# A sparse graph network on one core: the array of S in four instead of two, panels scattered twice, self-loop sums in PSUM

## The chip, the cores and the metric

The kernel runs on one core of one Trainium2 chip. The metric is the device time of one execution in microseconds. The core has a matrix engine (TensorE, PE in the profile, with its weight loads as PEld), a vector engine (VectorE, DVE), a scalar engine (ScalarE, ACT), a general engine (GpSimd, POOL) and a queue of transfers (SyncE, SP). POOL also issues the indirect transfers, which gather or scatter rows by a list of indices. Each engine works through its own instructions in order and waits at semaphores.

## The reference

Four layers over 32 sequences `x` of 512 nodes and 256 features, with one adjacency matrix `adj` (512 x 512, some 1.5% of it off zero, and the diagonal). Layers 0 and 3 are the costly ones, of this form (weights of their own):

```python
pre_u = einsum('bud,dk->buk', h_t, W1[:d])
pre_v = einsum('bvd,dk->bvk', h_t, W1[d:])
hidden = relu(pre_u[:, :, None, :] + pre_v[:, None, :, :] + b1)
S = sigmoid(einsum('buvk,ko->buvo', hidden, W2)[..., 0] + b2[0])
a_t = einsum('buv,bud->bvd', S * A_a, h_t)
m_t = einsum('uv,bud->bvd', A_m, h_t) * h_t
z_t = beta1*h_t + beta2*(a_t @ Wa + ba) + beta3*(m_t @ Wm + bm)
```

Layer 1 is `z + relu((adj @ z) @ W.T + b)`, layer 2 an attention over all nodes with `adj` added to the logits. `S` is multiplied by `adj`, so it is wanted only where `adj` is not zero.

## The kernel before

The kernel counts the edges of `adj` and takes a sparse path where they are few enough, as here. It works on groups of four sequences (`NB`), eight groups in all, and on the 512 nodes in four chunks of 128 rows (`NC`). For each group and each of the layers 0 and 3:

- `pre` (line 565) computes `pre_u` and `pre_v` with PE for each chunk, adds the bias (line 579, DVE), copies (580, ACT) and stores both to a `table` in DRAM, one row of 1024 numbers (four sequences) for each node and side. It also forms the sum for the node's edge to itself: line 582 adds both sides into the tile `both` in SBUF, line 583 takes relu, weights and sums to `self_s`.
- `edges` (line 616) takes the other edges in 36 items of 128 edges, one edge per partition. For each chunk there are eight items (`OWN`): the k-th edge of each row. Rows with more than eight edges put the rest into panels, two for each half of the rows (`PANELS`): lines of edges of any row in that half. For an item, POOL gathers the other node's rows (`rows`, line 612). The own node's rows (`mine`) come by one plain load for a chunk (line 652, SP) or, for a panel, by another gather (655). DVE adds the two (691), and then either DVE sums with relu and weights in four pieces (707) or DVE does relu and weights in one piece (699) and ACT sums (677). After every four items come exp (ACT, 597), the rest of the sigmoid (DVE, 601 and 602), the product with `adj` (641), and then one put for each item: POOL scatters 128 x 4 numbers to their places in `cells` (606).
- `cells` is the dense `S * adj` in DRAM, zeroed once. The edges stay the same for all groups, so the same places are written again. It is two arrays for each layer, one for each half of the rows (256 x 512 places of four sequences, then spare places for lanes that hold no edge). Consecutive puts into one array are ordered: a put waits until the last put into the same array has landed. `put` (665) picks the next ready item of the other half where there is one. The self loops go to the diagonal by one plain transfer for each half (636).
- `load` (726) reads `cells` back, 1 MB for each chunk, into the tiles `SA`; line 814 copies out one sequence at a time for PE (845) in layer 0, and line 1006 uses it in layer 3.

`middle` (793) is layer 0's end, layers 1 and 2 and the `pre` of layer 3 for the four sequences of a group, `last` (1021) the end of layer 3. The pieces of all these are woven together by times given in units of one `middle` (`weave` and `sparse_path`); while the middle of one group runs, the layer-3 edges of the last group and the layer-0 edges of the next one take turns. An `edges` fetches its first three items ahead (`LEAD`; five in the first and last group), and up to six more pieces (`TAIL`) put what is left at its end. Below that a scheduler fixes the order on each engine.

The order of the items (232 to 240): four of chunk 0, then pairs of chunks 0 and 2, 2 and 1, 1 and 3, and at the end chunk 3 by turns with the four panels. Three tiles hold `mine`. A tile can only be filled again when its last reader is done.

Of the kernel before, what the change touches and what calls it, by code (L numbers as in the profile page):

```python
# [16 lines left out]
P = 128  # L17
# [14 lines left out]
LEAD = 3  # L32
LEAD_AT_ENDS = 5
TAIL = 6
CELLS = HALF * N
ITEMS = NC * OWN + 2 * PANELS
SPARE = NC // 2 * OWN * P + LINES
GROUP = NB * D
HELD = 8

# [179 lines left out]
class Edges:  # L220
# [3 lines left out]
    def __init__(self, m, pool):  # L224
        nc = self.nc = m.nc
        self.m = m
        self.iu = pool.tile([P, 2 * PANELS], I32, name="iu")
        self.iv, self.cell = (pool.tile([P, ITEMS], I32, name=n) for n in ("iv", "cell"))
        self.value = pool.tile([P, ITEMS], F32, name="value")
        self.inode = pool.tile([P, 2 * PANELS], I32, name="inode")  # L230

        order = [item_of(0, j) for j in range(OWN // 2)]
        for lead, other in ((0, 2), (2, 1), (1, 3)):
            for j in range(OWN // 2):
                order += [item_of(lead, OWN // 2 + j), item_of(other, j)]
        tail = [panel_of(h, q) for h in range(2) for q in range(PANELS)]
        for j in range(OWN // 2):
            order.append(item_of(3, OWN // 2 + j))
            order += tail[j : j + 1]
        self.order = order  # L240

    def value_of(self, j):
        k = self.order.index(j)
        return self.value[:, k : k + 1]

    def half_of(self, j):
        return j // OWN // 2 if j < NC * OWN else (j - NC * OWN) // PANELS

    def build(self, counts, adjT, lists, psum, big, tmp):

# [3 lines left out]
        def sheet(n):  # L254
# [23 lines left out]
        nc.gpsimd.iota(row, [[0, 2], [P, 2]], 0, 1, allow_small_or_imprecise_dtypes=True)  # L278
        nc.vector.tensor_scalar(row, row, float(N), None, ALU.mult)
        spare = sheet(NC * OWN)  # L280
        nc.gpsimd.iota(
            spare, [[0, 2], [OWN * P, 2], [P, OWN]], CELLS, 1, allow_small_or_imprecise_dtypes=True
        )
        rows = []
        for _ in range(2):
# [30 lines left out]
        for c in (0, 2, 1, 3):  # L316
            if c == 1:

                pu = psum()[:, 0 : 2 * PANELS]
                ones_bf = bf2[:, 1024:1025]  # L320
                nc.vector.memset(ones_bf, 1.0)
                for k in range(2 * PANELS):
                    h, q = divmod(k, PANELS)
                    mm(nc, pu[:, k : k + 1], [(full[:, h * 2 + c, q * P : (q + 1) * P], ones_bf) for c in range(2)])
                u, node, slot, start, sp, vp, therep, tp = (sheet(2 * PANELS) for _ in range(8))
                nc.vector.tensor_scalar(u, pu, float(HALF - 1), None, ALU.min)
                nc.vector.tensor_copy(node, u)
# [6 lines left out]
                nc.vector.tensor_scalar(sp, slot, float(CELLS + NC // 2 * OWN * P), None, ALU.add)  # L334
# [51 lines left out]
    def slots(self, js, v, there, t, start, spare, off=None):  # L386
# [7 lines left out]
        if off is None:  # L394
            nc.vector.scalar_tensor_tensor(t, v, start, spare, ALU.add, ALU.subtract)
        else:
            nc.vector.tensor_tensor(t, v, start, ALU.add)
            nc.vector.tensor_tensor(t, t, spare, ALU.subtract)
        nc.vector.tensor_tensor(t, t, there, ALU.mult)
        nc.vector.tensor_tensor(self.cell[:, js], t, spare, ALU.add)  # L400

# [17 lines left out]
class Sparse:  # L419
# [3 lines left out]
    def __init__(self, ctx, m, counts, xr, outr, B):  # L423
# [4 lines left out]
        self.dram = pool("dram", 1, space=bass.MemoryType.DRAM)  # L428

        self.cells = {  # L430
            k: [self.dram.tile([CELLS + SPARE, NB], F32, name=f"cells_{k}{q}") for q in range(2)] for k in "03"
        }
        self.lists = self.dram.tile([N, 2 * N], F32, name="lists")
        self.x2s = self.dram.tile([B, P, NC, D], F32, name="x2s")
# [103 lines left out]

    def zeros(self, cells):
        for c in cells:  # L540
            flat = c[0:CELLS, :].rearrange("(q p a) b -> q p (a b)", q=4, p=P)
            for q in range(4):
                self.nc.gpsimd.dma_start(flat[q], self.zero)

    def setup_behind(self):
# [19 lines left out]
    def pre(self, g, b, hT):  # L565
# [3 lines left out]
        for c in range(NC):  # L569
# [8 lines left out]
            puv = self.small.tile([P, 2, D], F32, name="puv", bufs=3)  # L578
            nc.vector.tensor_tensor(puv[:, 0, :], pp[:, 0:D], w["b1bc"], ALU.add)  # L579
            nc.scalar.copy(puv[:, 1, :], pp[:, D:])  # L580
            both = self.small.tile([P, D], F32, name="both", bufs=1)
            nc.vector.tensor_tensor(both, pp[:, D:], puv[:, 0, :], ALU.add)
            nc.vector.scalar_tensor_tensor(
                both, both, 0.0, w["W2bc"], ALU.max, ALU.mult, accum_out=g.self_s[:, c, b : b + 1]
# [19 lines left out]
    def put(self, g, half, at, s):  # L604

        self.nc.gpsimd.indirect_dma_start(  # L606
            out=g.cells[half], out_offset=bass.IndirectOffsetOnAxis(ap=at, axis=0), in_=s, in_offset=None
        )

    def fetch(self, rows, g, at):  # L610
# [5 lines left out]
    def edges(self, g, spare=()):  # L616
# [12 lines left out]
        def own_1():  # L629
            self.sigmoid_of(own)  # L630
            diag = self.counts.diag.unsqueeze(2).to_broadcast([P, NC, NB])
            nc.vector.tensor_tensor(g.self_s, g.self_s, diag, ALU.mult)
            for q in range(2):
                diagonal = g.cells[q][q * HALF : q * HALF + HALF * (N + 1), :]
                diagonal = diagonal.rearrange("(c p a) b -> p c a b", p=P, a=N + 1)[:, :, 0, :]
                nc.sync.dma_start(diagonal, g.self_s[:, 2 * q : 2 * q + 2, :])

        def run_1(ks):
            self.sigmoid_of(g.s[:, ks, :].rearrange(flat))
# [1 line left out]
            nc.vector.tensor_tensor(g.s[:, ks, :], g.s[:, ks, :], value, ALU.mult)  # L641
            for k in range(ks.start, ks.stop):
                j = e.order[k]
                ready.append((e.half_of(j), e.cell[:, j : j + 1], g.s[:, k, :]))

        def fetch(n):
            j = e.order[n]
            c = j // OWN
            if c >= NC or c not in mine:
                t = self.gath.tile([P, GROUP], F32, name="mine", bufs=3)  # L650
                if c < NC:
                    nc.sync.dma_start(t, places[c, 0])
                    mine[c] = t
# [10 lines left out]

        def put():

            at = next((n for n, r in enumerate(ready) if r[0] != self.half), 0)
            if ready:
                r = ready.pop(at)
                self.half = r[0]  # L670
                self.put(g, *r)

        def sums(k, rows):
# [694 lines left out]
```

## Time and profile before

| | |
|---|---|
| timed runs | 3109.6 us median of 3 (3096.97 to 3116.11) |
| profiled execution | 3114.5 us, of which span 3112.8 us |
| PE busy | 2713.5 us (87%), mean granted clock 0.942 |
| DVE, ACT, POOL busy | 2302.9 (74%), 1337.7 (43%), 1531.2 (49%) |
| puts (line 606) | 576, 686.4 us busy, 747.0 us idle before them |
| gathers of rows (line 612) | 552 and 24, 667.6 and 33.2 us busy |
| DRAM traffic | 679 MB, 218 GB/s over the span |

The span runs from the first to the last instruction of the profiled execution; what lies around it is 1.7 us. "Idle before" is time in which the engine had nothing else to do, put down to what ended it. In the timelines of single engines each line has the start, the duration, the engine, the line of the kernel, the operation with its output and input, the number of merged instructions, and in brackets the idle time before it and what ended that.

### The profile page before, as it was taken

What the parts mean: (1) busy time and instruction counts of PE and PEld (TensorE: products, weight loads), DVE (VectorE), ACT (ScalarE), POOL (GpSimd) and SP (SyncE); (2) the same over time, 40 slices, a digit from 0 to 9 for tenths busy, and PEclk for the clock granted to TensorE, in tenths of its full rate; (3) what the DMA queues carried; (4) which work ended last, traced back from release to release, by engine and by line L of the source; (5) the groups of instructions that cost most, each with busy time, mean ns of one, the idle gap of its engine ahead of it and who ended that gap; (6) DMA issues with size and microseconds to landing.
All of it is one profiled execution on the core that took longest, in us unless ns stands there. A gap on an engine that the chain in (4) does not pass through costs nothing. (4 is left out here: it accounts for less than half of the span.)

```text
span 3112.8 us, 32475 instructions
## 1 busy us (share of the span) xinstructions
PE 2713.5 (87%) x8645; PEld 1639.7 (53%) x8646; DVE 2302.9 (74%) x6027; ACT 1337.7 (43%) x4101; POOL 1531.2 (49%) x1328
## 2 busy tenths in 40 slices
PE   6367878889998899989998899989998899879957
PEld 3133444446654566446654565545654466546636
DVE  6964877888689776988489785888679795772761
ACT  3553454444344433444354442544345343443440
POOL 2561553656345552656346562555436563450461
PEclk9688889999999999999999999999999999999979
DMA  8774657776778757776678766787578766551753
GB/s 278 267 238 151 210 164 242 248 261 214 225 214 293 220 189 227 245 263 216 210 212 258 236 196 211 243 266 234 177 225 273 247 220 200 182 183 49 231 196 115
DMA packets 302719, 679.40 MB, mean 218 GB/s; under 512 B 52672, under 2 KB 170944, under 8 KB 294336
## 3 DMA queue, kind: packets, MB, share of 16 engines
q0 software_dynamic: 122688, 414.40, 42.6%
q1 hardware_dynamic: 160880, 225.62, 22.0%
q10 hardware_dynamic: 18960, 37.24, 3.2%
q8 instruction: 70, 1.15, 0.1%
q14 instruction: 121, 0.99, 0.1%
HBM read 531.12 MB, written 146.01 MB: 218 GB/s over the span
## 5 line engine op out<-in xcount | busy, mean ns | idle before, releaser
L606 POOL DMA_INDIRECT cells<-s,cell x576 | 686.4, 1192 | 747.0 <-DMA cells<-s,cell 388.5
L612 POOL DMA_INDIRECT rows<-table,iv x552 | 667.6, 1209 | 619.9 <-DMA table<-puv 150.5
L691 DVE TENSOR_TENSOR rows<-rows,mine 128x1024 f32<-128x1024 f32 x552 | 667.4, 1217 | 191.7 <-DMA rows<-table,iv 173.3
L677 ACT ACTIVATE rows<-rows 128x256 f32<-128x256 f32 x1088 | 439.8, 407 | 506.6 <-DVE rows L699 477.3
L45 PE MATMUL pst<-adj,h 128*128 128x512 f32 x1024 | 452.6, 594 | 0.3 <-PE pst L946 0.3
L707 DVE SCALAR_TENSOR_TENSOR rows<-rows,L_gnn_W2bc 128x256 f32<-128x256 f32 x1120 | 415.0, 417 | 1.8
L45 PE MATMUL pst<-L_gnn_Wa,hT 128*128 128x256 f32 x1024 | 261.3, 406 | 104.8 <-DMA hT<-xT 56.2
L699 DVE SCALAR_TENSOR_TENSOR rows<-rows,L_gnn_W2bc 128x1024 f32<-128x1024 f32 x272 | 329.7, 1214 | 0.3
L45 PEld LDWEIGHTS pst<-adj,h 128*128 128x128 f32 x1024 | 193.4, 191 | 223.3 <-issue 219.4
L45 PEld LDWEIGHTS pst<-L_gnn_Wa,hT 128*128 128x128 f32 x1024 | 204.8, 205 | 151.8 <-issue 85.1
L45 PE MATMUL pst<-eT,feats 128*128 128x512 f32 x512 | 230.9, 604 | 13.0 <-ACT eT L958 13.0
L866 PE MATMUL pst<-WT,hT 128*128 128x256 f32 x512 | 155.1, 470 | 96.0 <-DVE hT L853 96.0
L45 PE MATMUL pst<-adjT,zW 128*128 128x512 f32 x512 | 227.7, 597 | 3.8 <-ACT zW L870 3.8
L1006 PEld LDWEIGHTS pst<-hWa,SA 128*128 128x128 f32 x896 | 213.8, 328 | 7.7 <-issue 4.1
L1006 PE MATMUL pst<-hWa,SA 128*128 128x256 f32 x896 | 216.8, 398 | 0.0
L814 ACT COPY flat<-SA 128x512 f32<-128x512 f32 x128 | 137.7, 1127 | 165.9 <-PE pst L45 83.7
L677 ACT ACTIVATION_READ_ACCUMULATOR rows<-rows 128x1 f32 x1088 | 205.4, 189 | 0.0
L845 PE MATMUL pst<-flat,hWa 128*128 128x512 f32 x448 | 196.8, 592 | 0.0
L866 PEld LDWEIGHTS pst<-WT,hT 128*128 128x128 f32 x512 | 121.4, 242 | 136.6 <-DVE hT L853 107.1
L579 DVE TENSOR_TENSOR puv<-pst,bc_L_gnn_b 128x256 f32<-128x256 f32 x256 | 104.4, 414 | 95.8 <-DMA table<-puv 58.6
L580 ACT COPY puv<-pst 128x256 f32<-128x256 f32 x256 | 93.5, 370 | 180.6 <-DVE puv L579 162.7
L45 PEld LDWEIGHTS pst<-eT,feats 128*128 128x128 f32 x512 | 97.2, 193 | 127.5 <-issue 109.4
(172 smaller groups left out, 3984.4 us busy)
## 6 DMA issues: line engine op xcount, KB each, us to landing
table<-puv SPq DMA_DIRECT2D x256, 256.0 KB, 5.7
SA<-cells POOLq DMA_DIRECT2D x64, 1024.0 KB, 7.2
h<-in_x_dram SPq DMA_DIRECT2D x64, 512.0 KB, 6.5
mine<-table SPq DMA_DIRECT2D x64, 512.0 KB, 5.5
hT<-xT SPq DMA_DIRECT2D x36, 512.0 KB, 5.0
h<-x2s SPq DMA_DIRECT2D x36, 512.0 KB, 4.4
xT<-hT ACTq DMA_DIRECT2D x32, 512.0 KB, 6.1
x2T<-yT SPq DMA_DIRECT2D x32, 512.0 KB, 5.5
```

Of the source, the lines that this page charges most:

```text
L45: nc.tensor.matmul(out, lhsT, rhs, start=(n == 0), stop=(n == len(pairs) - 1))
L579: nc.vector.tensor_tensor(puv[:, 0, :], pp[:, 0:D], w["b1bc"], ALU.add)
L606: self.nc.gpsimd.indirect_dma_start(out=g.cells[half], out_offset=bass.IndirectOffsetOnAxis(ap=at, axis=0), in_=s, in_offset=None)
L612: self.nc.gpsimd.indirect_dma_start(out=rows, out_offset=None, in_=g.table, in_offset=bass.IndirectOffsetOnAxis(ap=at, axis=0))
L677: self.behind(nc.scalar.activation(part, part, AF.Identity, accum_out=g.s[:, k, b : b + 1]))
L691: self.behind(nc.vector.tensor_tensor(rows, rows, other, ALU.add))
L699: nc.vector.scalar_tensor_tensor(by_entry, by_entry, 0.0, w2, ALU.max, ALU.mult)
L707: nc.vector.scalar_tensor_tensor(part, part, 0.0, w["W2bc"], ALU.max, ALU.mult, accum_out=at)
L814: self.nc.scalar.copy(flat[:, r, :], SA[r][:, :, b])
L845: nc.tensor.matmul(pz, hWa[:, r, cs], flat[:, r, :], start=(r == 0), stop=False)
L866: nc.tensor.matmul(pw[:, at], zT[:, d, cs], m.WT_1[:, d, :], start=(d + k == 0), stop=(d * k == 1))
L1006: nc.tensor.matmul(pz[:, k * D : (k + 1) * D], SA[r][:, cs, b], hWa[:, r, :], start=(r + k == 0), stop=False)
```

## The change

- Each layer's `cells` are four arrays, one for each chunk (128 x 512 places, then spare places). A put waits for the last put into the same chunk. `put` picks, among the ready ones, the array that was put to the longest ago.
- A panel's 128 lines can belong to either chunk of its half. It is put twice, once into each array, with a list of places for each (`cell` and `other_cell`); lanes that belong to the other chunk go to spare places. That makes 40 puts for the 36 items.
- The order of the items: four turns of chunk 0, three of chunks 0 and 2, one of 0, 2, 1, four of 2, 1, 3, one of 1, 3, the first panel, two of 1, 3, the last item of chunk 3, the other three panels.
- The diagonal takes four transfers instead of two. The zeros take as many transfers as before, of the same size.
- Four tiles for `mine` instead of three.
- `both` is no tile of its own any more: the self-loop sum is formed in the bank of PSUM that held `pre_u`.

```diff
-CELLS = HALF * N
+ROWS = P * N
+CELLS = ROWS + OWN * P + LINES
 ITEMS = NC * OWN + 2 * PANELS
-SPARE = NC // 2 * OWN * P + LINES
...
+        self.other_cell = pool.tile([P, 2 * PANELS], I32, name="other_cell")
+        self.lower = pool.tile([P, 2 * PANELS], F32, name="lower")
...
-        order = [item_of(0, j) for j in range(OWN // 2)]
-        for lead, other in ((0, 2), (2, 1), (1, 3)):
-            for j in range(OWN // 2):
-                order += [item_of(lead, OWN // 2 + j), item_of(other, j)]
-        tail = [panel_of(h, q) for h in range(2) for q in range(PANELS)]
-        for j in range(OWN // 2):
-            order.append(item_of(3, OWN // 2 + j))
-            order += tail[j : j + 1]
+        left = {c: [item_of(c, j) for j in range(OWN)] for c in range(NC)}
+        panels = [panel_of(h, q) for q in range(PANELS) for h in range(2)]
+        order = []
+        for turns, chunks in ((4, (0,)), (3, (0, 2)), (1, (0, 2, 1)), (4, (2, 1, 3)), (1, (1, 3))):
+            for _ in range(turns):
+                order += [left[c].pop(0) for c in chunks]
+        order.append(panels.pop(0))
+        while left[1]:
+            order += [left[1].pop(0), left[3].pop(0)]
+        order += left[3] + panels
...
+            upper, other = start, self.lower
+            nc.vector.tensor_tensor(other, there, self.lower, ALU.mult)
+            nc.vector.tensor_tensor(there, there, other, ALU.subtract)
+            nc.vector.scalar_tensor_tensor(upper, t, float(-ROWS), there, ALU.add, ALU.mult)
+            nc.vector.tensor_tensor(self.other_cell, upper, spare, ALU.add)
+            there = other
...
         self.cells = {
-            k: [self.dram.tile([CELLS + SPARE, NB], F32, name=f"cells_{k}{q}") for q in range(2)] for k in "03"
+            k: [self.dram.tile([CELLS, NB], F32, name=f"cells_{k}{q}") for q in range(NC)] for k in "03"
         }
...
-            flat = c[0:CELLS, :].rearrange("(q p a) b -> q p (a b)", q=4, p=P)
-            for q in range(4):
+            flat = c[0:ROWS, :].rearrange("(q p a) b -> q p (a b)", q=2, p=P)
+            for q in range(2):
...
-            both = self.small.tile([P, D], F32, name="both", bufs=1)
+            both = pp[:, 0:D]
             nc.vector.tensor_tensor(both, pp[:, D:], puv[:, 0, :], ALU.add)
...
-            for q in range(2):
-                diagonal = g.cells[q][q * HALF : q * HALF + HALF * (N + 1), :]
-                diagonal = diagonal.rearrange("(c p a) b -> p c a b", p=P, a=N + 1)[:, :, 0, :]
-                nc.sync.dma_start(diagonal, g.self_s[:, 2 * q : 2 * q + 2, :])
+            for c in range(NC):
+                diagonal = g.cells[c][c * P : c * P + P * (N + 1), :].rearrange("(p a) b -> p a b", a=N + 1)
+                nc.sync.dma_start(diagonal[:, 0, :], g.self_s[:, c, :])
...
-                ready.append((e.half_of(j), e.cell[:, j : j + 1], g.s[:, k, :]))
+                s, q = g.s[:, k, :], j - NC * OWN
+                if q < 0:
+                    ready.append((j // OWN, e.cell[:, j : j + 1], s))
+                else:
+                    ready.append((q // PANELS * 2, e.cell[:, j : j + 1], s))
+                    ready.append((q // PANELS * 2 + 1, e.other_cell[:, q : q + 1], s))
...
-                t = self.gath.tile([P, GROUP], F32, name="mine", bufs=3)
+                t = self.gath.tile([P, GROUP], F32, name="mine", bufs=4)
...
-            at = next((n for n, r in enumerate(ready) if r[0] != self.half), 0)
             if ready:
-                r = ready.pop(at)
-                self.half = r[0]
+                r = min(ready, key=lambda r: puts.index(r[0]))
+                ready.remove(r)
+                puts.append(puts.pop(puts.index(r[0])))
                 self.put(g, *r)
...
-        self.half = 1
+        puts = list(range(NC))
...
-            cells = g.cells[c // 2][c % 2 * P * N : (c % 2 + 1) * P * N, :]
+            cells = g.cells[c][0:ROWS, :]
```

More of the change, by code (lines that the diff above doesn't have):

```diff
@@ L229, in __init__ @@
         self.value = pool.tile([P, ITEMS], F32, name="value")
+        self.other_cell = pool.tile([P, 2 * PANELS], I32, name="other_cell")
+        self.lower = pool.tile([P, 2 * PANELS], F32, name="lower")
         self.inode = pool.tile([P, 2 * PANELS], I32, name="inode")
-        order = [item_of(0, j) for j in range(OWN // 2)]
-        for lead, other in ((0, 2), (2, 1), (1, 3)):
-            for j in range(OWN // 2):
-                order += [item_of(lead, OWN // 2 + j), item_of(other, j)]
-        tail = [panel_of(h, q) for h in range(2) for q in range(PANELS)]
-        for j in range(OWN // 2):
-            order.append(item_of(3, OWN // 2 + j))
-            order += tail[j : j + 1]
+        left = {c: [item_of(c, j) for j in range(OWN)] for c in range(NC)}
[8 more added lines that the diff above has]
+        order += left[3] + panels
+        assert len(order) == len(set(order)) == ITEMS
         self.order = order
@@ L244, in value_of @@
         return self.value[:, k : k + 1]
-    def half_of(self, j):
-        return j // OWN // 2 if j < NC * OWN else (j - NC * OWN) // PANELS
     def build(self, counts, adjT, lists, psum, big, tmp):
@@ L277, in build @@
         row = sheet(NC)
-        nc.gpsimd.iota(row, [[0, 2], [P, 2]], 0, 1, allow_small_or_imprecise_dtypes=True)
+        nc.gpsimd.iota(row, [[0, NC]], 0, 1, allow_small_or_imprecise_dtypes=True)
         nc.vector.tensor_scalar(row, row, float(N), None, ALU.mult)
@@ L281, in build @@
         nc.gpsimd.iota(
-            spare, [[0, 2], [OWN * P, 2], [P, OWN]], CELLS, 1, allow_small_or_imprecise_dtypes=True
+            spare, [[0, NC], [P, OWN]], ROWS, 1, allow_small_or_imprecise_dtypes=True
         )
@@ L333, in build @@
                 nc.vector.tensor_scalar(start, u, float(N), None, ALU.mult)
-                nc.vector.tensor_scalar(sp, slot, float(CELLS + NC // 2 * OWN * P), None, ALU.add)
+                nc.vector.tensor_scalar(self.lower, u, float(P), None, ALU.is_lt)
+                nc.vector.tensor_scalar(sp, slot, float(ROWS + OWN * P), None, ALU.add)
                 nc.vector.tensor_scalar(tp, slot, 1.0, None, ALU.add)
@@ L602, in sigmoid_of, with put @@
         self.nc.vector.reciprocal(t, t)
-    def put(self, g, half, at, s):
+    def put(self, g, c, at, s):
         self.nc.gpsimd.indirect_dma_start(
-            out=g.cells[half], out_offset=bass.IndirectOffsetOnAxis(ap=at, axis=0), in_=s, in_offset=None
+            out=g.cells[c], out_offset=bass.IndirectOffsetOnAxis(ap=at, axis=0), in_=s, in_offset=None
         )
```

## The prediction

> **What bounds the kernel now.** I read the page's busy row first, then the costliest groups, then busy time by stretches, then the timelines of POOL, DVE and PE where PE stands still.
>
> ```profile
> PE 2713.5 (87%) x8645; PEld 1639.7 (53%) x8646; DVE 2302.9 (74%) x6027; ACT 1337.7 (43%) x4101; POOL 1531.2 (49%) x1328
> L606 POOL DMA_INDIRECT cells<-s,cell x576 | 686.4, 1192 | 747.0 <-DMA cells<-s,cell 388.5
> L691 DVE TENSOR_TENSOR rows<-rows,mine 128x1024 f32<-128x1024 f32 x552 | 667.4, 1217 | 191.7 <-DMA rows<-table,iv 173.3
> ```
>
> PE is busy for 87%, so all that a change of the edge work can win is PE's remaining 400 us. The 576 puts (line 606) cost POOL 1.19 us each, and POOL stood 388.5 us before them because the previous put into the same array had not landed. DVE's add (line 691) waited 173 us for fetched rows. A period (one group) is some 358 us:
>
> ```profile
> 1050.00:1100.00 50.00, 50.00 (x175) 31.71 (x175) 44.58 (x112) 27.00 (x75) 31.16 (x26) 1.00 0.76 232
> 1300.00:1350.00 50.00, 42.56 (x129) 22.70 (x129) 46.28 (x150) 27.11 (x75) 31.07 (x25) 0.97 0.86 277
> 1350.00:1400.00 50.00, 40.77 (x111) 22.11 (x110) 36.94 (x92) 17.49 (x62) 26.57 (x25) 0.90 0.78 269
> ```
>
> (Window, length, then busy us of PE, PEld, DVE, ACT, POOL, granted clock, DMA share, GB/s.) At 1050 PE is full, whatever POOL waits for. It loses 9 us in 1350 to 1400, where a layer-3 group of edges ends and the next layer-0 group begins. There POOL's queue, DVE and PE read:
>
> ```profile
> 1327.88 1.50 POOL L606 DMA_INDIRECT cells<-s,cell  x1 [0.31 <-DVE puv L579]
> ...
> 1336.18 1.19 POOL L606 DMA_INDIRECT cells<-s,cell  x1 [5.42 <-DMA cells<-s,cell]
> ...
> 1343.40 1.09 POOL L606 DMA_INDIRECT cells<-s,cell  x1 [0.31 <-issue]
> ...
> 1351.02 0.97 POOL L606 DMA_INDIRECT cells<-s,cell  x1 [3.71 <-DMA cells<-s,cell]
> ...
> 1364.06 1.79 POOL L606 DMA_INDIRECT cells<-s,cell  x1 [3.88 <-DMA cells<-s,cell]
> ...
> 1369.24 1.19 POOL L606 DMA_INDIRECT cells<-s,cell  x1 [2.81 <-DMA cells<-s,cell]
> 1372.77 0.98 POOL L606 DMA_INDIRECT cells<-s,cell  x1 [2.34 <-DMA cells<-s,cell]
> 1374.05 1.01 POOL L612 DMA_INDIRECT rows<-table,iv  x1 [0.30 <-ACT hWa L745]
> ```
> ```profile
> 1380.31 1.23 DVE L691 TENSOR_TENSOR rows<-rows,mine 128x1024 f32<-128x1024 f32 x1 [8.75 <-DMA rows<-table,iv]
> ```
> ```profile
> 1382.19 6.58 PE L866 MATMUL pst<-WT,hT 128*128 128x256 f32 x16 [9.23 <-DVE hT L853]
> ```
>
> The waits in brackets, 5.42+3.71+3.88+2.81+2.34 = 18.2 us, hold back the new group's seventh fetch (1374.05); DVE stands 8.75 us for its rows, line 853 stands behind that add in DVE's queue, and PE 9.23 us behind line 853. The same stands at 674, 1023, 1740, 2098 and 2459: PE waits 6.8, 9.5, 9.2, 9.0, 5.0, 8.8, together 48.3 us. The start and the end of the kernel end on the same chain: last puts, load of S, matmul.
>
> ```profile
> 255.15 6.06 PE L845 MATMUL pst<-flat,big 128*128 128x512 f32 x10 [12.58 <-ACT flat L814]
> ```
> ```profile
> 3048.91 2.48 DMA cells<-s,cell
> 3052.16 2.10 DMA cells<-s,cell
> 3055.37 8.73 DMA SA<-cells
> 3064.15 7.77 PE pst L1006 x26
> ```
>
> **The change, part by part.** Sums are made against the profiled execution's 3114.5 us (span 3112.8 and 1.7 around it); the median of the three timed runs, 3109.6, is 4.9 lower, and I subtract from it.
>
> *More puts.* Each of 4 panels goes to two arrays: 40 puts a group for 36, 64 more in all, 1.19 and 0.30 of issue each: 6.0 us a group, 95 us of POOL. Where PE is full (1050 to 1150) this is hidden by PE's own work. It is not at the six changes of group, at the start and at the end, where POOL's queue decides.
>
> *Four arrays.* Which wait goes depends on what lies between two puts into one array. Old: from the last fetch of the old group (1324.85) to the seventh of the new (1374.05) are 22 instructions and 18.2 us of waits; (49.2-18.2)/22 = 1.41 us a step. New queue: 25 steps (four more puts, one own-row gather fewer), 35.3 us. Its puts go 0,3,1,3,1, two fetches, 3,1, fetch, 3,1, fetch, 2, fetch, 0,3,2,1, fetch, 3, load, 3, load, seventh fetch: the leftovers are chunks 1 and 3 by turns, so the chain of two arrays stays. I place each put no earlier than the landing of the previous one into its array, with the landings of the rows above in order (1327.88 to 1336.18 is 8.3 us; then 6.8 to 7.6; 5.2 at the end). Waits: 5.5, 1.1, 3.4, 1.1, 0.1, 3.0, sum 14.2. Total 49.5, less 1.0 because two of the steps are loads of 0.9 us: 48.5 against 49.2. With the queue behind it shorter by as much, a gain of 1 us per change, 6 in all. Bounds: all waits gone, the 48.3 us of PE's waits; none gone, three more steps, 6 x 4.2 = 25 us lost.
>
> Within a group three arrays by turns leave two other puts and a fetch between equal ones, over 4 us, so few waits stay. DVE's waits for rows between start and end sum to 144.6 us; 90.5 are eleven of 7 us and more at group boundaries, so some 50 are short ones. I take a third as put waits (17), half of it felt by PE, which waits for DVE in these stretches: -8 (bounds 0 and -25).
>
> *Start.* From the last own-row gather (209.41) old POOL needs 10 puts, 5 fetches, 4 loads and 16.2 us of waits until 249.1. New: 13 puts, 4 fetches, 4 loads, waits by the same placing 11: two steps more (+2.8), 5 less; and each array is loaded by itself, so that one copy of line 814 follows the last landing where two did (254.00 and 256.46): -2.5. Together -5 (bounds: all waits gone -12, no wait gone +6).
>
> *End.* The last three items are panels, so six puts stand at the end instead of a chain of half-1 puts (1.70, 3.69, 2.26 us of waits). After the last gather 17 puts for 12. The last item's data come sooner, since only one gather of own rows is left for the end where two were (DVE stood 8.4 us for one at 3026). Placed as above the last load goes at 3053.9 against 3055.4: -2 (bounds -9 by the waits of this end and its five more puts, +7 by the puts alone).
>
> *Four own-row tiles.* SP's loads and POOL's panel gathers wait less for a tile; POOL's 2.54 us at 919, 1276, 1636, 2356 is not followed by a PE wait: 0. Two more diagonal DMAs a group on SP (0.37 us of issue), queued ahead of table stores and loads; SP's wait for self_s is the same one: 0. The zeros are the same eight 512 KB writes a layer, and the second list of cells is six DVE instructions of 128x4 at some 0.17 us in a part of the setup that is off the chain: 0.
>
> *Self loops in PSUM.* Lines 582 and 583, 256 each, now write PSUM. No DVE row of this trace writes PSUM; rows that read it cost the same (579: 414 ns, 582: 417; 583 in SBUF: 418). I take 0 for the instruction, +2 us for the bank held until 583 (0.67 us longer at the places where PE waited for 582: 6.2 us in 3 times). Upper bound: 583 starts 0.46 us after 582, whose result it reads, the next independent instruction 0.35 us after 583 (1351.37, 1351.83, 1352.18); if a write to PSUM doubled that 0.11 us, 256 x 0.11 = 28 us of DVE, a third of it where PE waits for DVE, +9.
>
> [...]
>
> [...] The rows above land after 3.5 to 8.3 us. [...] I go by the rows.
>
> Sum: -6 -8 -5 -2 +2 = **-19 us**: 3095.5 on the profiled execution, **3090** on the median.
>
> **Rivals.**
> *The chain breaks altogether.* If landings shorten because fewer puts queue behind fetches, the six stalls (48), the short row waits (17), start (-12) and end (-8) go: 85, 3025. For it: 388.5 us of waits are there to be had. Against: chunks 1 and 3 alternate at the end as the halves did.
> *The longer queue decides (slower).* At each change of group POOL does four puts more ahead of the same fetches. If the waits stay as they were, 6.0 us a group come through six times and at both ends: +48, 3158. It decides from the point where the saved waits fall under the 4.2 us of three steps (I have 18.2-14.2 = 4.0 and 1.0 of shorter steps, so near it). For it: POOL's gaps there are bare 0.30 us, a full queue.
> *Nothing reaches PE.* PE is full over half the span; the stall is passed to the next wait for DVE (line 957 waited 41 us for line 918). 3110.
>
> **How the numbers follow.** Forecast 0.42, chain breaks 0.22, longer queue 0.18, nothing 0.18. The forecast alone spans 3065 to 3115. Measurement tells about 1% (31 us) from no change. Faster: the broken chain 0.22 and 0.28 of the forecast, 0.34. Slower: 0.17, nearly all of the longer queue. Same: 0.49. Range 3030 to 3145: it takes half of either rival.
>
> **What would show it.** After: 640 puts; waits of puts for puts down from 388 to 200-280 us; at the group change DVE's wait for rows 6 to 9 us and PE's wait for line 853's counterpart 7 to 9 us, six times; the two self-loop instructions within 10 ns of before; PE's first matmul of flat near 250; last load of S 1 to 3 us earlier against the end of the fetches. Wrong if those PE waits fall under 3 us (broken chain) or pass 13 (longer queue), or if the PSUM rows grow by 60 ns.

## The result, and the profile after

The changed kernel takes 3120.7 us (median of 18 runs, 3114.78 to 3131.11), the kernel before 3100.8 (18 runs, 3091.73 to 3116.11): ratio 1.0062, 95% interval 1.0049 to 1.0076. Run again later (e16), the ratio was 1.0053 (1.0032 to 1.0073). It is slower by some 0.6%, 20 us, where 20 us of gain were forecast. The profiled execution took 3129.4 us (span 3127.7) against 3114.5 (3112.8).

The page after has these lines:

```profile
PE 2725.3 (87%) x8645; PEld 1650.8 (53%) x8646; DVE 2305.5 (74%) x6032; ACT 1341.0 (43%) x4101; POOL 1595.6 (51%) x1392
L618 POOL DMA_INDIRECT cells<-s,cell x576 | 687.6, 1194 | 545.5 <-DVE s L652 193.0
L707 DVE TENSOR_TENSOR rows<-rows,mine 128x1024 f32<-128x1024 f32 x552 | 666.5, 1215 | 166.8 <-DMA rows<-table,iv 162.2
```

(Lines have moved: the put is 618 now, the fetch 624, the add 707, the matmul that stood behind line 853 is 882 behind 869.) POOL has 64 instructions and 64 us more. DVE's wait for rows is 11 us shorter. The waits of POOL (total us, times, longest) show that the four arrays did what they were made for:

```profile
POOL cells L618 <- DMA cells<-s,cell: 198.0, 96, 5.4
POOL rows L624 <- DVE rows L723: 155.6, 41, 27.7
...
POOL cells L618 <- DMA cells<-s,other_cell: 41.8, 12, 5.8
```

240 us of waits of puts for puts, where 388.5 were. PE gained nothing from it: it stood idle for 402.4 us of its span, against 399.3. The change of group that the prediction read at 1324 to 1382 is here, on POOL, DVE and PE:

```profile
1378.05 0.99 POOL L624 DMA_INDIRECT rows<-table,iv  x1 [0.30 <-issue]
1379.35 0.98 POOL L618 DMA_INDIRECT cells<-s,other_cell  x1 [0.30 <-issue]
1380.33 0.59 POOL L748 DMA_DIRECT2D SA<-cells  x1
1385.22 0.99 POOL L618 DMA_INDIRECT cells<-s,other_cell  x1 [4.30 <-DMA cells<-s,other_cell]
1386.21 0.58 POOL L748 DMA_DIRECT2D SA<-cells  x1
1387.10 1.03 POOL L624 DMA_INDIRECT rows<-table,iv  x1 [0.30 <-issue]
```
```profile
1395.94 1.22 DVE L707 TENSOR_TENSOR rows<-rows,mine 128x1024 f32<-128x1024 f32 x1 [6.68 <-DMA rows<-table,iv]
```
```profile
1399.32 2.93 PE L882 MATMUL pst<-WT,hT 128*128 128x256 f32 x6 [5.15 <-DVE hT L869]
```

Two second puts of panels stand between the fetches of 1378.05 and 1387.10, and the later of them waits 4.30 us for the landing of the earlier second put into its own array. Counting DVE's adds back from 1395.94, the one that waits 6.68 us takes the rows of the fetch at 1387.10; PE stands behind it.

The six changes of group together: PE's waits for line 869 are 5.8, 8.3, 5.2, 7.5, 10.2 and 12.7, sum 49.5 us, against 48.3. In the stretch from 58 to 6 us before each of them POOL waited 10.7 us (mean) for landings, against 18.3, and issued 16 puts, against 12: four puts at 1.1 and 0.3 of issue are 5.6 us.

At the start a load of S follows the last put into its array, and the second puts are last:

```profile
242.62 0.97 POOL L618 DMA_INDIRECT cells<-s,other_cell  x1 [0.30 <-issue]
...
249.50 1.00 POOL L618 DMA_INDIRECT cells<-s,other_cell  x1 [5.31 <-DMA cells<-s,other_cell]
...
253.16 0.54 POOL L748 DMA_DIRECT2D SA<-cells  x1 [1.52 <-DMA cells<-s,other_cell]
```

The last load goes at 253.16, against 249.1, and PE's first matmul of line 882 starts at 271.27, against 264.48. But the profile of e16, the same kernel again, has it 10.2 us earlier than this, and earlier than before (first after, then e16):

```profile
271.27 3.62 PE L882 MATMUL pst<-WT,hT 128*128 128x256 f32 x16
```
```profile
261.11 3.62 PE L882 MATMUL pst<-WT,hT 128*128 128x256 f32 x16
```

There too the second puts stand last and are waited for (3.70 and 4.58 us), so these waits are real, but one profile does not tell whether the start as a whole gained or lost. The end is as uncertain: from the first matmul of line 882 for the last sequence to the end of the span are 264.3 us (265.2 in e16), against 272.0, but e2, with the arrays, order and puts of before, has 265.6. Between start and end 15.9 us were lost (12.1 by e16's profile), and only 1.2 of them in the six waits above.

### The profile page after: what moved, and what is told of

It is laid out like the page before. It is cut to its first block, busy times and chain, and to the rows that moved or that the text cites. A ratio compares the mean times of both kernels' runs of the same rounds, so it can differ in the third digit from the quotient of the medians.

```text
span 3127.7 us, 32472 instructions
## 1 busy us (share of the span) xinstructions
PE 2725.3 (87%) x8645; PEld 1650.8 (53%) x8646; DVE 2305.5 (74%) x6032; ACT 1341.0 (43%) x4101; POOL 1595.6 (51%) x1392
## 5 line engine op out<-in xcount | busy, mean ns | idle before, releaser
L882 PE MATMUL pst<-WT,hT 128*128 128x256 f32 x512 | 162.1, 486 | 107.4 <-DVE hT L869 107.4
L47 PE MATMUL pst<-eT,feats 128*128 128x512 f32 x512 | 232.9, 609 | 12.7 <-ACT eT L974 12.0
```

The costliest lines, as they stand in the source:

```text
L47: nc.tensor.matmul(out, lhsT, rhs, start=(n == 0), stop=(n == len(pairs) - 1))
L882: nc.tensor.matmul(pw[:, at], zT[:, d, cs], m.WT_1[:, d, :], start=(d + k == 0), stop=(d * k == 1))
```

## The experiments

The kernel before took 3100 to 3122 us (medians) from one set of runs to another, so each kernel is compared by its ratio to the runs beside it. The columns behind the ratio are read from the profiles: PE's waits in the six changes of group, and POOL's waits for landings in the stretches before them, as above. They come from one profile each and spread: before, e1 and e2, alike in arrays, order and puts, have 48 to 55 us of PE's waits, and stretches that are counted from the start of PE's wait instead of its end give sums of landings up to 21 us different.

| | arrays | order | a panel is put | us | ratio (95%) | PE, six changes | landings |
|---|---|---|---|---|---|---|---|
| before | 2 | old | once | 3100.8 | 1 | 48.3 | 109.8 |
| changed | 4 | new | twice | 3120.7 | 1.0062 (1.0049-1.0076) | 49.5 | 64.0 |
| e1 | 2 | old | once | 3108.7 | 1.0007 (0.9982-1.0031) | 55.4 | 101.4 |
| e2 | 2 | old | once | 3098.9 | 0.9996 (0.9972-1.0019) | 49.0 | 104.8 |
| e3 | 4 | old | twice | 3171.6 | 1.0218 (1.0181-1.0254) | 79.6 | 90.7 |
| e4 | 4 | new | once | 3071.8 | 0.9899 (0.9866-0.9932) | 27.4 | 41.0 |
| e5 | 2 | new | once | 3149.0 | 1.0141 (1.0106-1.0176) | 74.7 | 82.2 |
| e6 | 4 | new | twice, aside | 3108.6 | 0.9999 (0.9978-1.0020) | 40.5 | 32.7 |
| e7 | 4 | new | twice | 3140.2 | 1.0129 (1.0066-1.0192) | 71.3 | 73.1 |
| e8 | 2 | old | once | 3124.0 | 1.0057 (1.0033-1.0081) | 64.7 | 100.1 |
| e9 | 4 | new | 6 puts of 4 | 3118.8 | 1.0012 (0.9979-1.0045) | 49.1 | 71.7 |
| e10 | 4 | new | 6 puts of 4 | 3127.3 | 1.0038 (1.0011-1.0065) | 51.0 | 43.2 |
| e11 | 4 | old | once | 3061.4 | 0.9808 (0.9760-0.9856) | 35.6 | 78.5 |
| e12 | 4 | new | twice | 3121.9 | 1.0017 (0.9993-1.0041) | 37.5 | 74.5 |
| e13 | 4 | old | twice, aside | 3126.2 | 1.0071 (1.0043-1.0098) | 56.0 | 53.2 |
| e14 | 4 | old | 6 puts of 4 | 3164.3 | 1.0192 (1.0130-1.0253) | 76.5 | 99.4 |
| e15 | 4 | old | 6 puts of 4 | 3187.5 | 1.0282 (1.0252-1.0311) | 79.8 | 109.6 |
| e16 | 4 | new | twice | 3118.4 | 1.0053 (1.0032-1.0073) | 47.3 | 64.7 |
| e17 | 4 | old | 5 panels, once | 3165.1 | 1.0145 (1.0120-1.0170) | 60.2 | 84.1 |
| e18 | 4 | old | 5 panels, once | 3161.4 | 1.0128 (1.0104-1.0151) | 64.4 | 61.2 |

**The self loops in PSUM, and the fourth tile (e1, e2).** Two small parts of the change, put into the kernel before.

```diff
-            both = self.small.tile([P, D], F32, name="both", bufs=1)
+            both = pp[:, 0:D]
...  (e2 also)
-                t = self.gath.tile([P, GROUP], F32, name="mine", bufs=3)
+                t = self.gath.tile([P, GROUP], F32, name="mine", bufs=4)
```

> The kernel before with one part alone: the self-loop sum in PSUM (both = pp[:, 0:D]). Theory P (the PSUM part costs what was measured): DVE's rows that write PSUM are longer (in the changed kernel 430 and 426 ns against 417 and 418, the read of the accumulator 139 against 80) and the bank is held longer, so this alone gives +10 to +20 us, ratio 1.003 to 1.006. Theory Q (POOL's longer queue is the cause): within 3 us of before, ratio 0.999 to 1.001. Theory O (the order of the items is the cause): the same, 0.999 to 1.001.

> The kernel before with the self-loop sum in PSUM and four own-row tiles, arrays and order as before. Theory P: +10 to +20 us from the PSUM part, the fourth tile gives 0 to -5. Theory Q and O: within 5 us of before; POOL's waits for a tile (33 us at the panel gathers) go down and PE does not feel it.

Neither makes a difference that these runs can tell. So PSUM does not explain the 0.6%.

**The order, and the second puts (e3, e4).** e3 takes the changed kernel back to the old order of items; e4 leaves the second put of each panel out, and with it those edges.

```diff
-                    ready.append((q // PANELS * 2 + 1, e.other_cell[:, q : q + 1], s))
```

> The changed kernel with the old order of the items (four arrays, panels put twice, four tiles, PSUM kept). Theory O (the new order, with three panels in a row at the end and own rows loaded earlier, is the cause): back to before, ratio 0.998 to 1.002. Theory Q (64 more puts in POOL's queue are the cause): as slow as the changed kernel or slower, 1.005 to 1.010, because the chunk-3 items at the end wait for each other and the extra puts are still there. Theory P: 1.003 to 1.006.

> The changed kernel without the second put of each panel: 36 puts a group instead of 40. It leaves out the edges of the panels that lie in the upper chunk of each half. Theory Q: the 20 us come back and more, 6 us at each of six changes of group and at both ends, ratio 0.985 to 0.998 to before. Theory O: as slow as the changed kernel, 1.004 to 1.008. Theory P: the same, 1.003 to 1.006.

Without the 64 second puts the kernel is 49 us faster than the changed one by the medians, 51 by the ratios (1.0062 to 0.9899), as theory Q said. The order is the same, and PE's waits in the six changes fall from 49.5 us to 27.4. At the start, where the changed kernel's last load of S goes at 253.16 (245.44 in e16), e4's goes here:

```profile
236.07 1.06 POOL L747 DMA_DIRECT2D SA<-cells  x2 [2.41 <-PE pst L47]
```

and at the change of group only the loads of S stand between two fetches, with waits of 2.32 and 0.64 us for landings, and no put:

```profile
1347.72 0.99 POOL L624 DMA_INDIRECT rows<-table,iv  x1 [0.30 <-issue]
1351.03 1.15 POOL L747 DMA_DIRECT2D SA<-cells  x2 [2.32 <-DMA cells<-s,cell]
1352.82 0.54 POOL L747 DMA_DIRECT2D SA<-cells  x1 [0.64 <-DMA cells<-s,cell]
1353.86 1.16 POOL L624 DMA_INDIRECT rows<-table,iv  x1 [0.49 <-issue]
```
```profile
1366.10 1.23 DVE L706 TENSOR_TENSOR rows<-rows,mine 128x1024 f32<-128x1024 f32 x1 [3.33 <-DMA rows<-table,iv]
```

6.1 us from fetch to fetch instead of 9.1, and DVE waits 3.3 us instead of 6.7. Not all of what POOL saves arrives: the fetch of 1353.86, whose rows this add takes, lands only 12.2 us after its issue, the one of 1387.10 in the changed kernel 8.8 us, the one of 1374.05 before 6.2 us. In these stretches the share of the DMA engines is 1.02, 0.95 and 0.64 (414, 309 and 146 GB/s): this fits a fetch that stands behind the loads of S in the transfers, now that POOL issues them closer together. What the transfers alone cost at a change was not tried.

Of the 50.7 us between the two spans 15.3 lie before the first matmul of line 882 (5.2 against e16's profile), 28.0 between that and the last sequence's (22.1 of them in the six changes), 7.4 in the end.

e3 went the other way than the theory that the new order does harm, and past every range: with the old order the changed kernel is 2.2% slower than the kernel before.

**What the order and the arrays are worth, and what a second put is made of (e5 to e8).** e5 is the kernel before with the new order, the fourth tile and PSUM. e6 sends the second puts to arrays of their own:

```diff
-                    ready.append((q // PANELS * 2 + 1, e.other_cell[:, q : q + 1], s))
+                    ready.append((q // PANELS * 2 + 1, e.other_cell[:, q : q + 1], s, True))
...
-            out=g.cells[c], out_offset=bass.IndirectOffsetOnAxis(ap=at, axis=0), in_=s, in_offset=None
+            out=(g.aside if aside else g.cells)[c], out_offset=bass.IndirectOffsetOnAxis(ap=at, axis=0), in_=s, in_offset=None
```

e7 and e8 let POOL put twice an item in every group, in the changed kernel and in the one before:

```diff
-            for _ in range(2 if spare and len(ready) > 2 else 1):
+            for _ in range(2 if len(ready) > 2 else 1):
```

> The kernel before (two arrays by halves, a panel put once) with the new order of items, the self loops' sums in PSUM and four tiles for own rows; only the four arrays and the second puts of the panels are missing. Theory A (the four arrays are worth about 30 us, which the second puts of the panels then eat): this one gets nothing of it, 3095 to 3115, ratio to the kernel before 0.998 to 1.005, and waits of puts for puts near 380 us. Rival B (the gain that e4 showed is the order's, not the arrays'): 3070 to 3085, ratio 0.990 to 0.995.

> The changed kernel, but the second put of each panel goes into an array of its own, one of four that nothing reads (so the edges of these puts are left out of the result). POOL issues the same 640 puts in the same places; only no put and no load of S waits for the 64. Theory T (the time of POOL for 64 puts more, 1.1 us each and 0.3 of issue, ahead of the fetches at a change of group and ahead of the loads of S at both ends): 3112 to 3125, ratio 1.004 to 1.008. Rival W (it is their waits: the second puts go into arrays whose last put has not landed, 116 us of waits before and behind them): near the kernel that puts panels once, 3072 to 3090, ratio 0.990 to 0.997. By the start of the changed kernel, where 4 puts are 5.6 us and the waits for them 6.8 of the 15 us lost, I expect about half way, 3095.

> The changed kernel, with two puts an item where more than two are ready in every group, not only in the first and the last: POOL issues the same 640 puts, earlier, in the middle of a group where PE is full. Theory L (the leftover puts of a group stand ahead of the next group's fetches, and that is where PE loses): the six waits of PE for line 869 fall from 49.5 us to 20 to 35, the time to 3090 to 3105, ratio 0.996 to 1.001; start and end are as before. Rival S (POOL's puts cost wherever they stand, by the waits for their arrays that now come closer together): 3118 to 3135, ratio 1.005 to 1.011, with more than 240 us of waits of puts for puts.

> The kernel before with the same edit alone. Theory L: the six waits of PE for line 853 fall from 48.3 us to 20 to 35, time 3075 to 3090, ratio 0.991 to 0.997. Rival S: with two arrays an earlier put waits for the one before it, POOL's waits grow past 400 us and push the fetches back within the group: 3100 to 3120, ratio 1.000 to 1.006.

e5: the new order in two arrays costs 1.4%, outside either range: the arrays were worth more than theory A gave them (1.0141 to 0.9899, 2.4% or 75 us), and the order by itself is a loss. e6 lies between its two theories: of the second puts' 1.63% some 1.00% (31 us) are POOL's time, 0.63% (20 us) the waits around them. The 31 us hold what the puts aside still wait for one another (19.5 us in the whole profile), and each part is good to about 12 us. e7 and e8 both lose, as rival S said, e7 more than its range. The profiles show why: what stands at the change of group is not a backlog. In the stretches before the six waits e7 still issues 92 puts (95 in the changed kernel), since by the code the last items' puts become ready only there; they wait more for one another (73 us for 64).

**Fewer second puts, and three tiles (e9, e10, e12).** In e9 and e10 the lines of a half's second chunk are laid from the end of the two panels, so that a half's first panel belongs to one chunk and is put once:

```diff
-            pairs = [(before, counts.lines[:, at])]
-            if c % 2:
-                pairs.append((ones[:, 0:P], counts.lines[:, c - 1 : c]))
-            mm(nc, pb[:, at], pairs)
+            mm(nc, pb[:, at], [(later if c % 2 else before, counts.lines[:, at])])
...
+                if q >= 0 and q % PANELS:
                     ready.append((q // PANELS * 2 + 1, e.other_cell[:, q : q + 1], s))
```

(`later` is `before` less one; the second chunk's `base` gets 256 more.) e9 also puts the twice-put panels ahead of the others. e12 is the changed kernel with `bufs=3` for `mine`.

> A version that computes everything: the changed kernel, with the lines of a half's second chunk laid from the end of its two panels, so that a half's first panel holds lines of its first chunk alone and is put once (the sparse path then needs a second chunk with at most 128 lines); 38 puts a group for 40 and 36. The twice-put panels stand between turns of chunks 1 and 3, the once-put ones last. By the 49 us that e4 gave for 64 puts, 32 puts fewer are worth 24 us: theory N (the number counts): 3090 to 3102 with the kernel before at 3104, ratio 0.995 to 0.999. Rival E (the puts that stand last count for more than the others, since every array's last put is what a load of S waits for): 3072 to 3088, ratio 0.990 to 0.995.

> The same, also computing everything, with the panels where the changed kernel has them: one early, three last, so that the last three items give five puts instead of six, and the early one gives one. Theory N: within 6 us of e9, 3090 to 3102, ratio 0.995 to 0.999. Rival E: 10 to 20 us above e9, ratio 0.997 to 1.003.

> The changed kernel with three tiles for own rows as before. Theory: the fourth costs and brings nothing, ratio 1.004 to 1.009 as the changed kernel. Rival: with the new order, in which three chunks run by turns, three tiles make SP's load or POOL's gather of own rows wait for a tile: ratio above 1.012.

The intervals of e9 and e10 overlap each other and that of e16, e10's also that of the changed kernel's first measurement: half of the second puts gone brought, by their middle values, 7 to 16 us, less than half of the 49. Neither beats the kernel before. e12 gave 1.0017 where 1.004 to 1.009 was expected; beside e16 (1.0053) the intervals still touch, so three tiles are no worse, and perhaps 0.4% better.

**The table's last corner (e11).** The changed kernel in the old order (e3) without the second puts.

> The changed kernel with four arrays, the old order of items, and each panel put once (the edges of the other puts are left out). Completes the table of order and arrays without second puts: two arrays and old order 1.000, two and new 1.014, four and new 0.990. Theory X (64 second puts cost 49 us in either order): 3115 to 3130, ratio 1.004 to 1.009; then four arrays alone bring nothing in the old order, and the new order alone loses: only together do they gain. Rival Y (the second puts cost more in the old order, whose panels alternate with chunk 3): 3080 to 3105, ratio 0.993 to 1.001.

0.9808: under both ranges. Four arrays in the old order are worth 1.9%, and the 64 second puts cost 4.1% there (127 us by 3100), not 1.6%.

**What the second puts cost in the old order (e13 to e16).** e13 is e6 with the old order, e14 is e10 with the old order and the twice-put panels first, e15 has these behind the third and fourth turn of chunks 1 and 3, e16 is the changed kernel again.

> Four arrays, the old order of items, each panel put twice, the second put into an array of its own that nothing reads (its edges are left out of the result). With the second puts into the real arrays 3172, without them 3061. Theory T (POOL's time for the 64 puts, 31 us in the new order, and the rest is waiting for arrays): 3085 to 3105, ratio 0.990 to 0.999. Rival C (in the old order POOL's queue is the full one at the end of a group and the time itself costs the 127 us): 3140 to 3175, ratio 1.010 to 1.022.

> A version that computes everything: four arrays, the old order of items, a half's second chunk laid from the end of its panels as in e9, so that two panels are put twice and two once; panels stand between the last four items of chunk 3 as before, the twice-put ones first. 32 second puts at 2.0 us each (127 us for 64) are 63 us: theory N 3110 to 3140, ratio 1.000 to 1.010. Theory C (what costs is the chain of the last puts into one array, and the last two panels are now put once): 3075 to 3100, ratio 0.988 to 0.998.

> The same, computing everything, with the twice-put panels further ahead, behind the third and the fourth turn of chunks 1 and 3, and the once-put ones behind the second and the fourth of the last four items of chunk 3. Theory C: at or below e14, 3070 to 3095, ratio 0.986 to 0.997. Theory N: as e14, 1.000 to 1.010. Rival: the last items of chunk 3 now stand two by two, and their puts wait for each other: above e14 by 10 to 20 us.

> The changed kernel once more, beside the kernel before on this chip: ratio 1.004 to 1.008 as measured. If it falls to 1.000 to 1.003, the ratio of three own-row tiles (1.002) and those of e9 and e10 say nothing against it.

e13 lies between its theories again: 2.6% (82 us, 1.3 us for each of 64 puts) is POOL's time, 1.5% the waits. e14 keeps half of the second puts and nearly all of the cost, and e15, with the same number in another order, is the slowest of all: the place counts, and the number alone does not tell the cost. e16 came out as expected. In e15 the last eleven items hold six of chunk 3 and a twice-put panel of its half, and the waits for landings before the six changes rise to 109.6 us. In the profile of e3 the wait at the changes looks like this:

```profile
1401.33 1.23 DVE L704 TENSOR_TENSOR rows<-rows,mine 128x1024 f32<-128x1024 f32 x1 [7.12 <-DMA rows<-table,iv]
1413.42 1.23 DVE L704 TENSOR_TENSOR rows<-rows,mine 128x1024 f32<-128x1024 f32 x1 [8.17 <-DMA rows<-table,iv]
```
```profile
1416.81 3.78 PE L879 MATMUL pst<-WT,hT 128*128 128x256 f32 x8 [15.74 <-DVE hT L866]
```

Two late fetches one behind the other, 15 us, where e11 has two waits of 2.6 and 3.9 us at the same place.

**No second put, one panel more (e17, e18).** Five panels, each of one chunk, each put once (two for chunk 0), in four arrays and the old order; e18 with three tiles.

```diff
-ITEMS = NC * OWN + 2 * PANELS
+PLACES = ((0, 0), (0, 1), (1, 0), (2, 0), (3, 0))
+ITEMS = NC * OWN + len(PLACES)
...
+                    ready.append((PLACES[q][0], e.cell[:, j : j + 1], s))
```

> A version that computes everything: four arrays, the old order of items, and five panels, each of one chunk (two of chunk 0, one of each other, the sparse path then needs at most 256 lines in chunk 0 and 128 in the others), so that each is put once: 37 items and 37 puts a group. Against e11 (3061, ratio 0.981) a group has one item more: two fetches, a put (4 us of POOL) and some 3 us of DVE, of it the part at a change of group and at the ends counts, the panel of chunk 3 standing further ahead. Theory C (each put that stands in the chain of the last puts costs, an item in the middle does not): 3065 to 3085, ratio 0.982 to 0.992. Rival N (POOL's time costs wherever it stands: 4 us by 8 groups and as much again by the waits): 3095 to 3125, ratio 0.995 to 1.005.

> As e17, computing everything, with three tiles for own rows as before. Theory (the fourth tile is worth nothing): within 6 us of e17. Rival (five gathers of own rows need it): 10 us and more above e17.

Theory C falls: e17 is 3.4% (105 us) slower than e11, more than rival N said. So it is not the chain into one array alone. This is no clean price of one item, though: the panels go to other arrays than in e11 (0, 1, 2, 0 among the last items, where e11 has 0, 0, 2, 2), and with 37 items one more of them goes to ACT and a batch of sigmoids near the end holds three items for two. Three tiles are as good as four.

A second place in each group is not in the table. Between the last sequence of one `middle` and the first of the next (from the first matmul of line 882, or its counterpart, of the one to that of the other) PE waits 1.7 us in e11, but 5.2 in e13, 5.7 in e14, 6.9 in e3 and 7.6 in e17 (means of six).

No kernel here that computes everything is faster than the one before; e1, e2, e9 and e12 can't be told from it.

## Why the prediction was wrong

It forecast 19 us of gain and got 20 of loss; that 3120.7 lies inside its wide range of 3030 to 3145 is no merit of the mechanism. Most of the signs that it named came (640 puts, 240 us of waits of puts for puts, PE's waits of 8 us in the mean at the changes), and the gain did not: they can't tell the terms apart. Three terms, none near its size, make the loss. By ratios of the runs, in the corner that the change took: four arrays -1.9% (e11), the new order +0.9% (e4 against e11), the second puts +1.6% (changed against e4); -60, +28 and +51 us of 3101, sum +19, measured +20. By the intervals the arrays' term is good to about 15 us, the order's to 18, the second puts' to 11. They hold for this path alone: in the old order the second puts cost 127 us, not 51.

- **"Four arrays", -6 and -8.** This step failed by its size: I let the chain of two arrays stay and gave the arrays 14 us between start and end, some 21 in all. They are worth 60 to 75 (e11; e5 to e4). The landings' waits at a change fell by 7.6 us, not by 4.0.
- **"More puts".** I wrote down 6.0 us a group and 95 us of POOL, then let three steps (4.2 us) into the sum at the changes and two (2.8) at the start only, against saved waits. This term failed too: the second puts cost 51 us, some 31 of POOL's time and 20 of the waits before and behind them (e6). That they stand where POOL's queue decides was said; that the second put is also the last one into its array, so that the next second put waits 4.3 to 5.3 us for it and the load of S 1.5 us (4.58 in e16), was not.
- **The new order had no term.** I counted what stands in the queue after it, put the rest at nothing without a reason and never asked what the order does by itself. It loses 1.4% in two arrays and 0.9% in four; only with the second puts does it help (e3 against the changed kernel, 1.6%). What in the order loses was not tried by itself, and the cause stays open. The profile offers, as candidates, the three panels at the end, whose gathers of own rows stand together, and POOL's wait for a row tile that DVE still reads, 155.6 us (82.6 before; 153.7 in e5).
- **Start, -5.** Not decided: +6.8 us in the profile after, -3.4 in e16's. The second puts cost something there: e4's start is 5.2 us earlier than e16's.
- **End, -2.** -7 to -8 by the two profiles: within its bounds, but e2's end, with no change to the puts, is 6.4 us shorter than before as well.
- **PSUM, +2.** Right within what e1 tells. The rows:

```profile
L594 DVE TENSOR_TENSOR pst<-pst,puv x256: 397/426/467, 30.5 to 2914.5; 128x256 f32<-128x256 f32 x128
...
L595 DVE SCALAR_TENSOR_TENSOR pst<-pst,L_gnn_W2bc x256: 405/423/467, 30.9 to 2915.0; 128x256 f32<-128x256 f32 x128
L595 DVE DVE_READ_ACCUMULATOR pst<-pst,L_gnn_W2bc x256: 129/140/144, 31.3 to 2915.3; 128x1 f32 x128
```

(ns, lowest, median, highest.) Before, the medians were 418, 417 and 81. The two instructions took 8 and 6 ns more, within the 10 ns that I allowed. The read of the accumulator took 59 ns more; at 40.51 and 1702.91 us, for instance, the next instruction starts together with it and does not wait.
- **The landings.** I went by the rows, 3.5 to 8.3 us. In the trace after, with a load of S issued between, puts still waited 4.30 us at 1385 and 5.31 us at 249.50, and the put of 1379.35 landed 5.6 us after its issue, within that range. The "chain breaks" rival needed shorter landings.
- **The rivals.** "The longer queue decides" is the one that came, though its price of 48 us stands against the 49 of the second puts and not against the whole; that the gain of the arrays lay beside it, it did not say. Its condition was wrong: the waits saved at a change (7.6 us) are more than the 5.6 us of four puts, and PE still gained nothing. "The chain breaks" came nearest to the size of the arrays' part (85 us, measured 60 to 75).

**Why PE follows POOL** is shown for the chain and not for the amounts. In every kernel the last wait of DVE over 1 us before the six stalls is for fetched rows, and ends 1.9 us (before), 3.4 us (after) or at most 5.2 us (e18) ahead of PE's. Within one order, from e11 to e3, 13 more puts (18 us) and 12 us of landings in POOL's queue stand against 44 us more of PE's waits; from e4 to the changed kernel 23 puts (32 us) and 23 us of landings against 22. But from the changed kernel to e10, 19 puts and 21 us of landings fewer brought PE nothing (51.0 us against 49.5). The time of the transfers, as in e4 above, is a rival to POOL's queue that no run separates.

**Open**: why the old order bears so little. From e11 every addition cost 80 us or more: 64 puts aside (82), 32 second puts (119), a fifth panel (105). A sum of single prices doesn't give that, nor do the six changes alone, which hold 20 to 41 us of each; the second place in the group holds 21 to 35 more. The corner e11 rests on one set of four runs.

## What to carry to other kernels

A change of several parts wants a price for each of them alone, the reordering as well, and a measurement of the corners of the table: here terms of -60, +28 and +51 us lay behind a difference of 20, and the last was 127 in the other order. A part of the kernel read from one profile wants a second profile of the same kernel: here the start differed by 10 us between two. In POOL's queue an added put cost its own time, here 1.1 us and 0.3 of issue, and made a new last landing, for which the next second put waited 4.30 and 5.31 us and the load of S 1.52; count both at every place where the queue decides. And before work is pulled forward, look whether it is ready earlier: the puts at a change of group were not.

## What was not expected of the hardware

In each of the six stalls of PE at the changes of group in the profile after, the granted clock fell to 0.50, and the sixteen matmuls of line 882 behind the stall took 5.92 to 6.76 us, against 3.62 at 271.27 with the full clock, so that such a wait cost more than itself. Around the change of group after (window, length, busy us of PE, PEld, DVE, ACT, POOL, granted clock, DMA share, GB/s):

```profile
1380.00:1390.00 10.00, 10.00 (x24) 4.39 (x24) 9.26 (x25) 4.38 (x15) 5.08 (x6) 1.00 0.91 244
1390.00:1400.00 10.00, 4.85 (x16) 2.87 (x15) 4.03 (x11) 1.50 (x7) 5.02 (x7) 0.85 1.00 355
1400.00:1410.00 10.00, 10.00 (x32) 7.15 (x31) 9.23 (x23) 4.34 (x15) 4.48 (x4) 0.81 0.91 330
1410.00:1420.00 10.00, 10.00 (x31) 5.59 (x30) 10.00 (x24) 4.37 (x18) 7.26 (x8) 1.00 0.73 233
```

After a wait of 5.15 us the clock is 0.81 for the next 10 us, then full. In windows of 0.5 us it is 0.50 from 1397.0 to 1403.5 and full from 1404.0, that is, it falls some 3 us after PE stopped (1394.2) and is back 4 to 5 us after PE went on (1399.3). Over the runs the mean clock is higher in the fastest of these kernels and lower in the slow ones: 0.948 in e4 (3072 us), 0.942 in the kernel before, 0.932 in e3 (3172 us). PE's busy time for the same matmuls is 2713.8 us in e4 and 2735.7 in e3, 22 us of the 101 between their spans; but it is no rule that a slower kernel has more of it: the kernel before has 2713.5.
